# A selective scan in longer chains: units of 16 channels by 8 states over 1024 tokens, two halves in a row, with the B and C rows loaded once and ten product tiles

## The chip, the cores and the metric

The kernel runs on one core of one Trainium2 chip. The metric is the device time of one execution in microseconds (us); lower is better. The engines are named as in the profile: PE (TensorE, the matmuls), PEld (its weight loads), DVE (VectorE), ACT (ScalarE), POOL (GpSimd) and SP (SyncE, which here only issues DMAs).

## The reference

Four images of 64x64 tokens with 128 channels pass through four layers. The layer that matters here is the first, a selective scan: the tokens of an image are read in four orders (k = 0 to 3: by rows, by columns, and both backwards), and for each order, each of 256 channels and each of 16 states a recurrence runs over all 4096 tokens.

```python
xs    = stack([x0, x1, x0[..., ::-1], x1[..., ::-1]])      # 4 orders, 256 channels, 4096 tokens
delta = softplus(dts + dt_b)                               # one number per order, channel, token
A     = -exp(A_log)                                        # per order, channel, state
def step(h, t):
    x_t, d_t, B_t, C_t = t
    h = exp(d_t[..., None] * A) * h + (d_t * x_t)[..., None] * B_t[:, :, None, :]
    return h, einsum('bkdn,bkn->bkd', h, C_t)              # sum over 16 states
_, ys = scan(step, h0, (xs, delta, Bs, Cs))
ys    = ys + Ds * xs                                       # then the four orders are added up
```

After it come a layer norm, a gate and a projection, an MLP, and three more layers (attention, convolutions, neighbourhood attention with an MLP). They are called "the rest" below, and they are not changed.

## The kernel before

**Work of the scan.** `scan_inputs` makes `delta`, `du` = delta * x and the B and C rows of an image and stores them to DRAM, one block for each order and each of 8 chunks of 512 tokens. `selective_scan` then goes through an image: four orders, 8 chunks, two halves `hf` of the channels, four groups `j` of 4 states, and two units `pp`: 512 units in an image, 2048 in all. A unit holds 32 channels by 4 states on the 128 partitions, and two channel groups `g` side by side, each over 512 tokens. Its steps are:

- L468: SP loads `dt` and `du` (512 KB each, a row of a channel broadcast to its 4 states; four buffers each; one pair of tiles serves four units). L478: SP loads `b_rows` and `c_rows` (256 KB each, broadcast to 32 channels; four buffers each) for each `hf` and `j`.
- L485: POOL multiplies `dB = du * B`, 128x1024, into one of four buffers.
- L491: ACT takes the exponential, 128x512, into a PSUM tile `dA`, one for each `g`; there are three such tiles.
- L493: DVE runs the recurrence, `tensor_tensor_scan`, 128x512, for each `g`. It begins from zero in the first chunk of an order and from a column of the tile `state` in the others. The two scans of a unit have nothing to do with each other.
- The product with C. In 9 of 16 units (11 of 16 in the first image) the scan is written back into `dA` and DVE multiplies it into a product tile `hc` (L498), once for each `g`. In the others (`on_pool`, chosen by the tuple `ON_POOL`) the scan is written into `hc` and POOL multiplies in place, 128x1024 (L506), two units later in the program (`BEHIND`). There are six `hc` tiles.
- The last column of the scan is copied to `state` by ACT for the next chunk: twice in a unit of the first kind (L500), once in the second (L502), and not at all in the last chunk of an order.
- L539: PE sums the states with the matrix `pick`: four matmuls for each pair of units into a PSUM tile `py`. Only this frees an `hc` tile. After four pairs ACT copies `py` to `y_sum` (L549, L556) and issues its store (L552, L558).

**Order of the work.** Each engine works through its own list of instructions in order. The lists are made when the kernel is built, by a scheduler that plays the program through and takes, for each engine, what would be ready, by priority. The scan of image 0 runs beside `scan_inputs` of the later images, the scan of image n beside the rest of image n-1, and the rest of the last image runs alone at the end. The rest uses PE and ACT most, DVE a little, POOL hardly at all.

The lines that set the buffers of the scan:

```python
dB = pool.tile([128, 2, LC], F32, name="dB", bufs=4)
nc.gpsimd.tensor_mul(dB, dus[pp], mid(bt, 2))
hc = pool.tile([128, 2, LC], F32, name="hc", bufs=6)
dA = psum.tile([128, LC], F32, name="dA", bufs=3)
```

Of the kernel before, what the change touches and what calls it, by code (L numbers as in the profile page):

```python
# [45 lines left out]
NPR, NJS = 4, NS // 4  # L46
# [10 lines left out]
SCAN_FIRST = 10_000_000  # L57

# [63 lines left out]
def make_consts(ctx, tc):  # L122
# [9 lines left out]
    K.mhalf = pool.tile([128, 128], F32, name="mhalf")  # L132
    nc.gpsimd.memset(K.mhalf, -0.5)
# [143 lines left out]
def scan_inputs(tc, K, A, D, img):  # L277
# [5 lines left out]
    with ExitStack() as ctx:  # L283
# [12 lines left out]
        def steps(o, c):  # L296
# [26 lines left out]
            for b in range(2):  # L323
                k, first = o + 2 * b, 64 * b + 1 + R
                nc.scalar.dma_start(D.bc[img][k][c].rearrange("n w t -> w n t"), xdbl[first : first + 2 * NS, :])
                nc.scalar.dma_start(D.delta[img][k][c], deltas[b])
                du = pool.tile([128, ND, LC], F32, name="du")
                nc.gpsimd.tensor_mul(  # L328
                    du.rearrange("p d (a b) -> p d a b", b=H),
                    deltas[b].rearrange("p d (a b) -> p d a b", b=H), tk,  # L330
                )
                nc.sync.dma_start(D.du[img][k][c], du)
# [77 lines left out]
def make_scan(ctx, tc, K, A):  # L410
# [7 lines left out]
    S.A = load("A_log", [128, KD, NJS, NPR, 2])  # L418
    nc.scalar.activation(S.A, S.A, AF.Exp)
    nc.vector.tensor_scalar_mul(S.A, S.A, -1.0)  # L420
    ds4 = load("Ds", [128, ND, KD])
    total = big.tile([128, ND], F32, name="Dsum")
    nc.vector.tensor_reduce(total, ds4, AX.X, ALU.add)
    S.skip = big.tile([128, ND, 128], F32, name="skip_diag")
    for d in range(ND):
        nc.scalar.activation(S.skip[:, d, :], K.ident, AF.Copy, scale=total[:, d : d + 1])

    S.pick = big.tile([128, 32], F32, name="pick")
    nc.gpsimd.memset(S.pick, 1.0)
    for base, sign in ((0, 1), (3, -1)):  # L430
        nc.gpsimd.affine_select(
            S.pick, S.pick, [[-4 * sign, 32]], ALU.is_ge, 0.0, base=base, channel_multiplier=sign
        )
    S.unit = 0
    return S


def selective_scan(tc, K, S, D, img):

# [9 lines left out]
    for k in ORDER:  # L455
        back = k >= 2
        order = slice(None, None, -1) if back else slice(None)
        last = 0 if back else LC - 1
        state = pool.tile([128, NJS, NPR, 2], F32, name="state")
        for i in range(NCH):  # L460
            c = NCH - 1 - i if back else i
            for hf in range(2):
                dts, dus = [], []
                for pp in range(2):
                    rows = span(2 * hf + pp, 32)
                    for name, src, out in (("dt", D.delta, dts), ("du", D.du, dus)):
                        t = pool.tile([128, 2, LC], F32, name=name, bufs=4)
                        nc.sync.dma_start(  # L468
                            t.rearrange("p g t -> p (g t)"),
                            src[img][k][c][rows].rearrange("d g t -> d (g t)").unsqueeze(1).to_broadcast([32, 4, 2 * LC]),  # L470
                        )
                        out.append(t)
                py = []
                for j in range(NJS):

                    bt, ct = (pool.tile([128, LC], F32, name=name, bufs=4) for name in ("b_rows", "c_rows"))
                    for w, t in enumerate((bt, ct)):
                        nc.sync.dma_start(  # L478
                            t, D.bc[img][k][c][4 * j : 4 * j + 4, w, :].unsqueeze(0).to_broadcast([32, 4, LC])
                        )  # L480
                    hcs, made = [], []
                    for pp in range(2):
                        pr = 2 * hf + pp
                        dB = pool.tile([128, 2, LC], F32, name="dB", bufs=4)
                        nc.gpsimd.tensor_mul(dB, dus[pp], mid(bt, 2))  # L485
                        on_pool = S.unit % 16 in ON_POOL[img > 0]
                        S.unit += 1
                        hc = pool.tile([128, 2, LC], F32, name="hc", bufs=6)
                        for g in range(2):
                            dA = psum.tile([128, LC], F32, name="dA", bufs=3)  # L490
                            nc.scalar.activation(dA, dts[pp][:, g, :], AF.Exp, scale=S.A[:, k, j, pr, g : g + 1])  # L491
                            hg = hc[:, g, :] if on_pool else dA
                            nc.vector.tensor_tensor_scan(  # L493
                                hg[:, order], dA[:, order], dB[:, g, order],
                                0.0 if i == 0 else state[:, j, pr, g : g + 1], ALU.mult, ALU.add,
                            )
                            if not on_pool:
                                mm = nc.vector.tensor_mul(hc[:, g, :], dA, ct)  # L498
                                if i < NCH - 1:
                                    nc.scalar.copy(state[:, j, pr, g : g + 1], dA[:, last : last + 1])  # L500
                        if on_pool and i < NCH - 1:
                            nc.scalar.copy(state[:, j, pr, :], hc[:, :, last])  # L502
                        if on_pool:

                            def product(hc=hc, ct=ct, made=made):
                                made.append(nc.gpsimd.tensor_mul(hc, hc, mid(ct, 2)))  # L506

                            waiting.append((S.unit + BEHIND, product))
                        else:
                            made.append(mm)  # L510
                        hcs.append(hc)
                        settle(S.unit)

                    def total(k=k, c=c, hf=hf, j=j, hcs=hcs, made=made, py=py):
                        if j == 0:
                            py.append(psum.tile([128, LC], F32, name="py"))
                            before = pool.tile([128, LC], F32, name="y_before", bufs=3)
                            if k == 0:
                                for pp in range(2):
                                    nc.sync.dma_start(  # L520
                                        before[span(pp, 64), :],
                                        D.xc[img][c][span(2 * hf + pp, 32)].rearrange("d g t -> g d t"),
                                    )
                                nc.tensor.matmul(py[0], S.skip[:, hf, :], before, start=True, stop=False)
                            elif k >= 2:
                                nc.sync.dma_start(before, D.y_first[img][k % 2][c][:, hf, :])
                                nc.tensor.matmul(py[0], K.ident, before, start=True, stop=False)
                            if k == 2:
                                cols = pool.tile([128, NCH, RC, RC], F32, name="y_before", bufs=3)
                                nc.sync.dma_start(  # L530
                                    cols.rearrange("p c a b -> p c (a b)"),
                                    D.y_cols[img][:, :, c, hf].rearrange("c p x -> p c x"),
                                )
                                nc.tensor.matmul(
                                    py[0].rearrange("p (a c b) -> p a c b", a=RC, b=RC), K.ident,
                                    cols.rearrange("p c a b -> p a c b"), start=False, stop=False,
                                )
                        for q in range(4):
                            mm = nc.tensor.matmul(  # L539
                                py[0][32 * q : 32 * q + 32, :], S.pick, hcs[q // 2][:, q % 2, :],  # L540
                                start=(k == 1 and j == 0), stop=(j == NJS - 1),
                            )
                            if q == 0:
                                for m in made:
                                    after(tc, mm, m)
                        if j == NJS - 1:
                            y = pool.tile([128, LC], F32, name="y_sum")
                            if k == 3:
                                nc.scalar.copy(  # L549
# [5 lines left out]
                            else:  # L555
                                nc.scalar.copy(y, py[0])  # L556
                                to = D.y[img][c] if k == 2 else D.y_first[img][k % 2][c]
                                nc.scalar.dma_start(to[:, hf, :], y)  # L558

                    waiting.append((max([S.unit] + [w[0] for w in waiting]), total))  # L560
                    settle(S.unit)
    settle(S.unit + BEHIND)


# [299 lines left out]
def make_layer2(tc, K, A, D, pool):  # L864

    nc = tc.nc

    def fold(out, raw, rows, width):  # L870

# [885 lines left out]
```

## Time and profile before

| what | value |
|---|---|
| device time, median of 3 runs (lowest to highest) | 8911.95 us (8906.75 to 8919.55) |
| span of the profiled execution | 8926.7 us, 14.7 us above that median |
| busy: PE, DVE, ACT, POOL | 7138.8, 7119.8, 5642.5, 7048.6 us |
| first scan of image 0, 1, 2, 3 begins at | 125, 2202, 4080, 5942 us |
| last scan ends, rest of the last image alone | 7795 us, then to 8927 us |
| scans on DVE (L493) | 4096 |
| products on DVE (L498), on POOL (L506) | 2432, 832 |
| ACT copies of states (L500, L502) | 2128 of 158 ns, 728 of 190 ns |

A row of the table of groups reads: line, engine, operation, tiles written and read, shape, count, then the busy time with the mean of one instruction, then the idle time of the engine just before them with what ended most of it. A row of the table of stretches gives the stretch, its length, and the busy time of each engine in it. In the timeline "x2" joins two instructions that follow each other.

### The profile page before, as it was taken

To read this page: it belongs to the slowest core of one execution; us is meant where nothing else is said; L and a number is where in the kernel's file an instruction comes from. 1 tells how busy PE (TensorE), PEld (TensorE's weight loads), DVE (VectorE), ACT (ScalarE), POOL (GpSimd) and SP (SyncE) were. 2 spreads that over 40 slices of the span, in tenths; PEclk is the share of its full clock that TensorE was granted. 3 is DMA by queue.
4 is the path that set the end of the run, shared out by engine and by line. 5 is a ranking of instruction groups with operands and counts; after the bars stand their busy time and mean duration, and the time that the engine had idled before them with its cause. 6 is when DMAs were issued, how large, how long until landed. Compare 5 with 4: busy or idle time off the path is not lost. (4 is left out here: it accounts for less than half of the span.)

```text
span 8926.7 us, 101201 instructions
## 1 busy us (share of the span) xinstructions
PE 7138.8 (80%) x30116; PEld 2711.7 (30%) x30116; DVE 7119.8 (80%) x8483; ACT 5642.5 (63%) x11581; POOL 7048.6 (79%) x3064
## 2 busy tenths in 40 slices
PE   6835868687788997887788988777888888888987
PEld 2211213132332232333322232333322333343333
DVE  3888878888899989998899989988999889813433
ACT  5646767676576666667766666657766666654355
POOL 5988898989899989998899979987899889900000
PEclk8756868697799998888899998888899988999989
DMA  5777676777554546566444555565544555520020
GB/s 174 249 236 239 227 252 239 266 240 266 188 168 165 170 150 222 188 205 201 164 165 164 179 180 195 191 208 171 166 167 169 169 198 194 173 69 4 7 79 29
DMA packets 864124, 1581.89 MB, mean 177 GB/s; under 512 B 219702, under 2 KB 344781, under 8 KB 859214
## 3 DMA queue, kind: packets, MB, share of 16 engines
q1 hardware_dynamic: 733261, 1399.17, 47.0%
q10 hardware_dynamic: 130304, 176.19, 5.5%
q8 instruction: 240, 3.93, 0.2%
q14 instruction: 319, 2.61, 0.1%
HBM read 1280.47 MB, written 283.59 MB: 175 GB/s over the span
## 5 line engine op out<-in xcount | busy, mean ns | idle before, releaser
L485 POOL TENSOR_TENSOR dB<-du,b_rows 128x1024 f32<-128x1024 f32 x2048 | 4801.3, 2368 | 622.9 <-DVE hc L493 184.8
L491 ACT ACTIVATE dA<-dt,w_A_log 128x512 f32<-128x512 f32 x4096 | 2784.7, 690 | 636.5 <-DVE hc L493 353.1
L493 DVE TENSOR_TENSOR_SCAN dA<-dA,state,dB 128x512 f32<-128x512 f32 x2128 | 2634.8, 1272 | 231.0 <-ACT dA L491 136.3
L493 DVE TENSOR_TENSOR_SCAN hc<-dA,state,dB 128x512 f32<-128x512 f32 x1456 | 1802.5, 1268 | 263.6 <-PE py L539 117.2
L506 POOL TENSOR_TENSOR hc<-hc,c_rows 128x1024 f32<-128x1024 f32 x832 | 1969.3, 2367 | 52.7 <-issue 23.9
L498 DVE TENSOR_TENSOR hc<-dA,c_rows 128x512 f32<-128x512 f32 x2432 | 1567.9, 676 | 115.0 <-PE py L539 97.5
L539 PE MATMUL py<-hc,pick 128*32 128x512 f32 x8192 | 1244.7, 686 | 367.3 <-POOL hc L506 270.7
L500 ACT COPY state<-dA 128x1 f32<-128x1 f32 x2128 | 327.5, 158 | 1220.4 <-DVE hc L498 1211.8
L829 PE MATMUL pa<-e,l_v 128*128 128x512 f32 x2048 | 1062.0, 650 | 16.8 <-ACT e L785 16.2
L781 PE MATMUL pair<-l_g,l_f 32*128 32x512 f32 x2048 | 530.5, 667 | 198.3 <-ACT e L785 146.9
L785 ACT ACTIVATE e<-pair 128x1024 f32<-128x1024 f32 (+1 forms) x448 | 508.4, 1135 | 225.7 <-PE pair L781 220.3
L829 PEld LDWEIGHTS pa<-e,l_v 128*128 128x128 f32 x2048 | 374.2, 199 | 668.5 <-issue 621.1
L539 PEld LDWEIGHTS py<-hc,pick 128*32 128x32 f32 x8192 | 209.5, 116 | 1114.7 <-issue 476.7
L247 PE MATMUL ps<-band,w_conv_diag 128*128 128x504 f32 (+3 forms) x1152 | 503.5, 596 | 6.7 <-ACT delta L397 6.5
L1287 PE MATMUL pair<-table,ident 128*128 128x512 f32 x768 | 414.3, 665 | 111.4 <-ACT e L1297 79.1
L493 DVE TENSOR_TENSOR_SCAN dA<-dA,dB 128x512 f32<-128x512 f32 x304 | 356.2, 1213 | 76.2 <-POOL dB L485 57.4
L328 POOL TENSOR_TENSOR du<-delta,xc 128x1024 f32<-128x1024 f32 x128 | 335.4, 2630 | 52.0 <-ACT delta L397 45.3
L1297 ACT ACTIVATE e<-pair 128x1024 f32<-128x1024 f32 (+1 forms) x224 | 254.3, 1135 | 155.6 <-PE pair L1291 155.6
L201 PE MATMUL ps<-ident,ln_xn 128*128 128x128 f32 x512 | 134.2, 360 | 263.9 <-ACT ln_xn L198 214.3
L219 PE MATMUL ps<-xnT,w_fc_w 128*128 128x512 f32 x512 | 266.6, 656 | 62.9 <-ACT xnT L202 22.7
L233 PE MATMUL ps<-mlp_h,w_fc_w 128*128 128x512 f32 x512 | 275.8, 683 | 42.6 <-ACT mlp_h L226 42.6
L247 PEld LDWEIGHTS ps<-band,w_conv_diag 128*128 128x128 f32 x1152 | 221.6, 194 | 288.7 <-issue 260.4
(274 smaller groups left out, 8400.0 us busy)
## 6 DMA issues: line engine op xcount, KB each, us to landing
b_rows<-bc_dram SPq DMA_DIRECT2D x1024, 256.0 KB
c_rows<-bc_dram SPq DMA_DIRECT2D x1024, 256.0 KB
dt<-delta_dram SPq DMA_DIRECT2D x512, 512.0 KB
du<-du_dram SPq DMA_DIRECT2D x512, 512.0 KB
delta_dram<-delta ACTq DMA_DIRECT2D x128, 512.0 KB
du_dram<-du SPq DMA_DIRECT2D x128, 512.0 KB
table<-biasT_dram SPq DMA_DIRECT2D x72, 512.0 KB
y_first_dram<-y_sum ACTq DMA_DIRECT2D x128, 256.0 KB
```

What stands on the lines that cost most here:

```text
L247: mm = nc.tensor.matmul(out[:, r0 - row0 : r1 - row0, c0:c1], lhsT((dy + 1) * 3 + dx + 1), src[:, r0 + dy : r1 + dy, c0 + dx : c1 + dx], s ...
L328: nc.gpsimd.tensor_mul(du.rearrange("p d (a b) -> p d a b", b=H), deltas[b].rearrange("p d (a b) -> p d a b", b=H), tk,)
L485: nc.gpsimd.tensor_mul(dB, dus[pp], mid(bt, 2))
L491: nc.scalar.activation(dA, dts[pp][:, g, :], AF.Exp, scale=S.A[:, k, j, pr, g : g + 1])
L493: nc.vector.tensor_tensor_scan(hg[:, order], dA[:, order], dB[:, g, order], 0.0 if i == 0 else state[:, j, pr, g : g + 1], ALU.mult, ALU.add,)
L498: mm = nc.vector.tensor_mul(hc[:, g, :], dA, ct)
L506: made.append(nc.gpsimd.tensor_mul(hc, hc, mid(ct, 2)))
L539: mm = nc.tensor.matmul(py[0][32 * q : 32 * q + 32, :], S.pick, hcs[q // 2][:, q % 2, :], start=(k == 1 and j == 0), stop=(j == NJS - 1),)
L781: nc.tensor.matmul(ps[:, u, :], f[quad, t // 4, span(t % 4, 128)], g[quad, c, :], start=True, stop=True)
L785: made = nc.scalar.activation(e, ps, AF.Exp)
L829: nc.tensor.matmul(pa, v[:, 8 * q + t, :], es[q], start=(t == 0 and q == 0), stop=(t == 7 and q == 3),)
L1287: nc.tensor.matmul(ps[:, u, :], K.ident, t[:, u, :], start=True, stop=False)
```

## The change

The unit keeps its size, 128x1024, but takes another cut: 16 channels by 8 states on the partitions and 1024 tokens of one channel group in a row. The two scans of a unit are now two halves of one chain: the second begins from the last column of the first, read where the first scan wrote it (`dA` or `hc`), and one ACT copy to `state` stands at the end of a unit, in three of four chunks (there are now four chunks of 1024 tokens in an order). `dt` and `du` tiles are 1 MB, two buffers each, and serve four units as before. `b_rows` and `c_rows` are 512 KB, loaded once in a chunk for each half of the states, with as many buffers as are in use at one time (two). `ON_POOL` is read with the unit's number counted from one instead of zero. From the second image on, after its first 40 units, four more product tiles come from a pool of their own (`widen`). The matrix `pick` has two variants, `y` tiles hold one group of channels over 1024 tokens, and their blocks in DRAM follow; the stores of `y` of orders 3 and 2 and the loads of `y_cols` go in two DMAs of 64 partitions instead of one of 128. The constant `mhalf` moves into the function that uses it.

```diff
-NPR, NJS = 4, NS // 4
+NPR, NSUB, NSH = 4, 2, 2
+LONG = 2 * LC
+NLG = NT // LONG
+HC, MORE, DB = 6, 4, 4
...
+class Products:
+    def widen(self, pool):
+        self.wider, self.more, self.turn = pool, True, -40
+    def tile(self):
+        self.turn += 1
+        if self.more and self.turn > 0 and self.turn % (HC + MORE) < MORE:
+            return self.wider.tile([128, LONG], F32, name="hc", bufs=MORE)
+        return self.pool.tile([128, LONG], F32, name="hc", bufs=HC)
...
-                        t = pool.tile([128, 2, LC], F32, name=name, bufs=4)
+                            t = pool.tile([128, 2, LONG], F32, name=name)
...
-                    bt, ct = (pool.tile([128, LC], F32, name=name, bufs=4) for name in ("b_rows", "c_rows"))
+                            if pr == 0 and a == 0:
+                                rows[h] = [pool.tile([128, LONG], F32, name=m, bufs=2) for m in ("b_rows", "c_rows")]
...
+    def run(x):
+        S.unit += 1
+        on_pool = S.unit % 16 in ON_POOL[img > 0]
+        x.dB = pool.tile([128, LONG], F32, name="dB", bufs=DB)
+        nc.gpsimd.tensor_mul(x.dB, x.du, x.b)
+        x.hc = S.products.tile()
...
+        start = 0.0 if x.first else x.state
+        for part in range(2):
+            at = span(1 - part if x.back else part)
+            dA = psum.tile([128, LC], F32, name="dA", bufs=3)
+            nc.scalar.activation(dA, x.dt[:, at], AF.Exp, scale=x.scale)
+            h = x.hc[:, at] if on_pool else dA
+            nc.vector.tensor_tensor_scan(
+                h[:, order], dA[:, order], x.dB[:, at][:, order], start, ALU.mult, ALU.add
+            )
+            if not on_pool:
+                x.made.append(nc.vector.tensor_mul(x.hc[:, at], dA, x.c[:, at]))
+            start = h[:, last : last + 1]
+        if not x.final:
+            nc.scalar.copy(x.state, start)
...
-        for name, shape in (("delta", [128, ND, LC]), ("du", [128, ND, LC]), ("bc", [NS, 2, LC])):
+        for name, shape in (("delta", [128, ND, 2, LC]), ("du", [128, ND, 2, LC]), ("bc", [NS, 2, 2, LC])):
...
+                    S.products.widen(scan_ctx.enter_context(tc.tile_pool(name="ss_more", bufs=1)))
```

## The prediction

> **What bounds the kernel now.** I read the table of stretches first, cut where the first scan of each image and of each order begins, because the busy shares of the whole span mix the scan with the 1122 us in which the rest runs alone. Three of the twelve stretches of images 1 to 3:
>
> ```profile
> core 0: us, PE busy (x) PEld busy (x) DVE busy (x) ACT busy (x) POOL busy (x), PEclk, DMA share, GB/s
> 4080.00:4577.00 497.00, 399.44 (x1618) 171.55 (x1610) 435.60 (x553) 362.14 (x780) 426.25 (x184) 0.87 0.51 169
> 4577.00:5010.00 433.00, 387.56 (x1559) 114.17 (x1560) 403.14 (x430) 285.71 (x544) 428.19 (x186) 0.93 0.48 166
> 5010.00:5491.00 481.00, 418.97 (x1750) 151.44 (x1752) 428.97 (x500) 310.93 (x634) 425.02 (x184) 0.90 0.57 188
> ```
>
> In the second POOL works 428 of 433 us: POOL sets its length. In the others POOL has the same work but idles 56 to 71 us; DVE idles 52 to 61 us. So two engines are nearly full. Summed over images 1 to 3 (5603 us), DVE idles 577 and POOL 470 us. In image 0 (2077 us) POOL is busy 1866 and DVE 1718.
>
> The groups say what fills them:
>
> ```profile
> L485 POOL TENSOR_TENSOR dB<-du,b_rows 128x1024 f32<-128x1024 f32 x2048 | 4801.3, 2368 | 622.9 <-DVE hc L493 184.8
> L493 DVE TENSOR_TENSOR_SCAN dA<-dA,state,dB 128x512 f32<-128x512 f32 x2128 | 2634.8, 1272 | 231.0 <-ACT dA L491 136.3
> L493 DVE TENSOR_TENSOR_SCAN hc<-dA,state,dB 128x512 f32<-128x512 f32 x1456 | 1802.5, 1268 | 263.6 <-PE py L539 117.2
> L500 ACT COPY state<-dA 128x1 f32<-128x1 f32 x2128 | 327.5, 158 | 1220.4 <-DVE hc L498 1211.8
> ```
>
> POOL waits mostly for DVE (a `dB` tile comes free when its scan is done), so DVE is the later of the two outside the POOL-bound stretches. The waits of images 1 to 3 (2202 to 7805 us) show what holds DVE:
>
> ```profile
> DVE hc L493 <- PE py L539: 96.5, 59, 5.7
> DVE hc L493 <- ACT dA L491: 81.8, 58, 4.5
> DVE ps L943 <- ACT ps L939: 80.3, 20, 5.4
> DVE dA L493 <- ACT dA L491: 77.8, 65, 5.1
> DVE hc L498 <- PE py L539: 37.0, 30, 3.6
> DVE dA L493 <- POOL dB L485: 32.1, 24, 3.9
> ```
>
> 134 us are waits for a product tile, 160 for an exponential, 80 are the rest's own. Only 44 (32 and 12) are for POOL.
>
> **The part that I hold decisive: neighbours on DVE.** The timeline shows how closely DVE instructions follow each other:
>
> ```profile
> 3203.16 1.28 DVE L493 TENSOR_TENSOR_SCAN dA<-dA,state,dB 128x512 f32<-128x512 f32 x1
> 3204.53 0.69 DVE L498 TENSOR_TENSOR hc<-dA,c_rows 128x512 f32<-128x512 f32 x1
> 3205.14 1.28 DVE L493 TENSOR_TENSOR_SCAN dA<-dA,state,dB 128x512 f32<-128x512 f32 x1
> 3206.46 0.69 DVE L498 TENSOR_TENSOR hc<-dA,c_rows 128x512 f32<-128x512 f32 x1
> 3207.06 2.45 DVE L493 TENSOR_TENSOR_SCAN hc<-dA,state,dB 128x512 f32<-128x512 f32 x2
> 3209.43 2.44 DVE L493 TENSOR_TENSOR_SCAN dA<-dA,state,dB 128x512 f32<-128x512 f32 x2
> ```
>
> A product that reads the scan just in front of it starts 1.37 and 1.32 us after that scan started. Two independent scans start 1.19 us apart (2.37 for two): the second begins before the first has ended. Over the whole trace the medians are 1.325 us (251 dependent pairs) and 1.175 us (1116 scans followed by a product of another tile), so a dependent neighbour costs 0.15 us. The list before mostly has scan, scan, product, product, so few neighbours depend on each other. In the list of the changed kernel, as built, a scan is followed at once by its own product 1734 times instead of 251, and in units for POOL by the second half of its own chain 529 times instead of 0, because the second half needs the first. The second kind is not in the trace; the nearest row gives 1.325 against 1.19 us, 0.135 us, with 0 and 0.3 as ends. Images 1 to 3: (1289 - 120) x 0.15 + 441 x 0.135 = 175 + 60 = +235 us of DVE time. Image 0: (445 - 131) x 0.15 + 88 x 0.135 = +59 us.
>
> How much lies on the path: in the four stretches that POOL sets (2710, 4577, 6460, 7377), DVE idles about 30 us of 430 and 103 of the 235 us fall there; I take half as covered, -51. The cover is POOL's own 2.33 us per instruction; where a DVE stall opens it is gone, and all 103 count. In image 0 POOL is busier than DVE, and I count half, +30.
>
> A rule speaks against this term. The Trainium skill, "VectorE: DVE Perf Modes", section "The DRAIN you can't avoid", says that the next operation waits for the pipe to empty anyway and that a semaphore between chained operations costs nothing extra. By it the 235 and 59 us would be 0 and the sum 8837 us. The rows above disagree by 0.15 us in each pair, and I take the rows.
>
> **Product tiles.** Ten instead of six, after image 1's first 40 units: of the 134 us for tiles between 0 and all can go. Products and scans that carry a wait on PE fall from 1852 to 1435 in the lists, a fifth; I take half of the time, -67. Image 0 keeps six and its 83 us.
>
> **State copies.** ACT loses 2128 + 728 copies (466 us) and gains 1536 at 158 ns (243 us): -223 us. It gains 64 store issues of 0.52 and 64 of 0.33 us, +54. ACT is 73% busy in these images and idled 1371 us in front of the copies, so only what comes late to DVE counts: 160 us for exponentials and 22 for states in images 1 to 3. The three `dA` tiles do not become more, and a first half's tile is now held until its second half is scanned, so I take a quarter of the 160 and half of the 22, -51 (ends: 0, -182). Image 0: -15 of its 108. In the second half 1216 scans read their start from PSUM, which no row shows; a start from `state` against none costs 60 ns (1272, 1213), so +-60 ns, +-73 us; I take 0, as it is a pointer read in both.
>
> **Loads.** `dt` and `du` double to 1024 MB together (a row goes to 8 partitions instead of 4), B and C fall from 512 to 128 MB. By the trace's packet medians (2 KB 84, 4 KB 159, 8 KB 309 ns) over 16 engines the loads take 326 + 2531 = 2857 us instead of 1376 + 1303 = 2679, two points of a share of 0.53 (0.71 in image 0): hidden. But rows have no spare buffer. At each chunk the first new C tile waits for the last product of the old one, and behind it on SP's queue stand `dt` and `du`. Landing took 4.4 us in the median for 256 KB and 5.0 for 512 KB; DVE has about two units, 6 to 7 us, before it needs the tile. POOL needs the second B tile after two `dB`, 4.7 us. So 0 to 5 us at each of 48 chunks, 0 to 240; I take 1, near the lower end, as most is covered: +48, and +10 for the 16 of image 0.
>
> **Nothing.** Scans, products, exponentials, POOL multiplications and matmuls stay as many and as large. Two more 393 ns copies, two 213 ns selects and the moved constant lie before the first scan at 125 us; stores of `delta` and `du` in 2 KB packets add 18 us of DMA time over 2077. If the DMAs were full these would be bare. The rest after 7805 us stays.
>
> **Sum.** Images 1 to 3: 235 - 51 - 67 - 51 + 48 = +114. Image 0: 30 - 15 + 10 = +25. Together +139 us on the span of 8926.7, and on the median of 8911.95, which is 14.7 lower: 9051 us.
>
> **The rivals.**
> - *Faster: the stalls shrink by more than DVE gains.* If all waits for tiles, exponentials, states and POOL go (134 + 160 + 22 + 44 = 360) against +235, images 1 to 3 fall by 125: 8787 us. It decides from 235 us of stalls saved, 41% of DVE's 577 idle. For it: ten tiles, 223 us less on ACT. Against: 80 us are the rest's, and `dA` stays at three. Chance 0.32, 8700 to 8890.
> - *Much slower: the rows arrive late.* A full landing of 5 us at all 64 chunks costs 320 instead of 58: 9313 us. Against: the cover above. Chance 0.12, 9200 to 9450.
> - *No difference:* within 0.2% (18 us, about what a measurement of this kernel can tell from no change). The terms cancel, 8912 us. Chance 0.06.
> - *Forecast:* 8935 to 9200, chance 0.50.
>
> **The numbers.** Slower 0.50 + 0.12 = 0.62, same 0.06, faster 0.32. The range goes from 8820 to 9290: it leaves out about a tenth at either side. The forecast's own range is 8935 to 9200.
>
> **What would show it.** Right: DVE's product after its scan starts 1.33 us behind it in most pairs, second halves for POOL units likewise; DVE's waits on PE's `py` below 70 us in images 1 to 3; POOL waits more for DVE; the stretches that POOL set get longer than 433 us. Wrong: second halves start 1.19 us after the first; the images get shorter than 1862 us although DVE's neighbours cost 0.15 us each; or DVE and POOL wait for `c_rows` and `b_rows` for hundreds of microseconds.

## The result: slower by 8.6%, and the profile after

| kernel | device time, median (lowest to highest) | ratio to before, 95% interval |
|---|---|---|
| before | 8915.75 us (8906.75 to 8920.03) | 1 |
| changed | 9689.83 us (9676.61 to 9698.3) | 1.0862, 1.085 to 1.0875 |

The direction of the forecast was right and the size was wrong: +774 us instead of +139, outside the range of 8820 to 9290 us. The profiled execution has a span of 9693.4 us. Cut at the first scan of each image, the time went here (times from the trace, in us, counted, like the first scans in the table before the prediction, from a point 11 us before the first instruction):

| | first scan at | image 0 | images 1 to 3 | last scan at | from there to the end |
|---|---|---|---|---|---|
| before | 125 | 2077 | 5603 | 7804 | 1134 |
| changed | 178 | 2211 | 6164 | 8553 | 1151 |
| difference | +53 | +134 | +561 | +749 | +17 |

The views count from the first instruction itself. So every stretch here and in the prediction begins and ends some 11 us after the scan that it is named for, and the rest of the last image ran alone for 1133 us of the span before, not 1122. The differences are not touched by this.

The table of stretches for the same orders of image 2 as were shown of before. Columns: the stretch, its length, the busy time of each engine, the granted clock of PE, the DMA share and GB/s.

```profile
core 0: us, PE busy (x) PEld busy (x) DVE busy (x) ACT busy (x) POOL busy (x), PEclk, DMA share, GB/s
4457.00:4986.00 529.00, 413.39 (x1627) 178.21 (x1626) 436.68 (x557) 355.74 (x694) 426.08 (x184) 0.85 0.75 175
4986.00:5466.00 480.00, 391.75 (x1540) 116.67 (x1544) 422.54 (x434) 277.55 (x465) 429.58 (x186) 0.88 0.71 168
5466.00:5998.00 532.00, 429.07 (x1726) 152.06 (x1718) 437.94 (x489) 297.23 (x537) 424.93 (x183) 0.87 0.78 183
```

POOL has its 425 to 430 us of work as before, but the stretch that it filled (433 us) now takes 480. DVE works 423 of them. Neither engine is full any more. The DMA share rose from about 0.5 to 0.75, and the GB/s did not rise with it.

The waits of DVE and then of POOL in images 1 to 3 (2389 to 8553 us; columns: total, times, longest):

```profile
DVE hc L585 <- DMA c_rows<-bc_dram: 450.2, 52, 26.5
DVE hc L581 <- ACT dA L579: 90.9, 57, 8.3
DVE dA L581 <- POOL dB L571: 70.3, 28, 14.4
DVE dA L581 <- ACT dA L579: 44.3, 34, 5.6
```

```profile
POOL dB L571 <- DVE dA L581: 228.8, 77, 18.5
POOL dB L571 <- DMA du<-du_dram: 214.2, 77, 12.5
POOL dB L571 <- DMA b_rows<-bc_dram: 207.7, 47, 19.1
```

Both engines now wait for DMAs. DVE waits for C rows for 450 us in 52 waits, 8.7 us each, about once in each of the 48 chunks. POOL waits 422 us for `du` and B rows. Before, POOL waited 2.9 us for `du` and 2.4 us for B rows in these images. The waits for a product tile are gone from the top of DVE's list, as forecast.

The groups on the changed lines (columns as before: busy time, mean ns, idle time ahead with what ended most of it):

```profile
L571 POOL TENSOR_TENSOR dB<-du,b_rows 128x1024 f32<-128x1024 f32 x2048 | 4793.5, 2358 | 1228.3 <-DVE dA L581 319.7 <-DMA du<-du_dram 272.6 <-DMA b_rows<-bc_dram 239.0
L579 ACT ACTIVATE dA<-dt,w_A_log 128x512 f32<-128x512 f32 x4096 | 2798.3, 690 | 2423.7 <-DVE dA L581 1885.1 <-DVE hc L581 372.0 <-DMA dt<-delta_dram 44.0
L585 DVE TENSOR_TENSOR hc<-dA,c_rows 128x512 f32<-128x512 f32 x2432 | 1662.3, 687 | 713.5 <-DMA c_rows<-bc_dram 520.6 <-PE py L518 85.0 <-DVE dA L581 2.3
L581 DVE TENSOR_TENSOR_SCAN hc<-dA,hc,dB 128x512 f32<-128x512 f32 x832 | 1064.9, 1280 | 140.2 <-ACT dA L579 88.7 <-DVE hc L581 1.4
```

No instruction got slower by more than a few per cent (POOL 2368 to 2358 ns, the scan 1268 to 1280, the product 676 to 687). What changed is the idle time ahead of them. The timeline of DVE shows the neighbours that the prediction was about (columns: start, duration):

```profile
3209.08 1.29 DVE L581 TENSOR_TENSOR_SCAN dA<-dA,dB 128x512 f32<-128x512 f32 x1
3210.40 0.69 DVE L585 TENSOR_TENSOR hc<-dA,c_rows 128x512 f32<-128x512 f32 x1
3211.01 1.27 DVE L581 TENSOR_TENSOR_SCAN hc<-dA,state,dB 128x512 f32<-128x512 f32 x1
3212.39 1.28 DVE L581 TENSOR_TENSOR_SCAN hc<-dA,hc,dB 128x512 f32<-128x512 f32 x1
3213.59 1.27 DVE L581 TENSOR_TENSOR_SCAN dA<-dA,state,dB 128x512 f32<-128x512 f32 x1
```

A product starts 1.32 us after its own scan, a second half 1.38 us after its first half, and a scan of another chain 1.20 us after the scan in front of it. Over the whole trace the medians are 1.322 (1734 products), 1.379 (529 second halves) and 1.174 to 1.199 us for independent neighbours.

The last view is the page's table of DMA queues (columns: packets, MB, share of the span of 16 engines); q1 is the queue with the scan's loads, first before, then after:

```profile
q1 hardware_dynamic: 733261, 1399.17, 47.0%
```

```profile
q1 hardware_dynamic: 492621, 1533.28, 65.5%
```

Ten per cent more bytes in a third fewer packets took 18 points more of the DMA time. In the trace, the 8 KB packets of images 1 to 3 (`dt` and `du`) take 608 ns in the median. The 4 KB packets, now nearly all of B and C rows, take 261 ns; before, those were nearly all of `dt` and `du` and took 159. A load of `dt` lands 7.4 us after its issue instead of 4.7, `du` 10.9 instead of 6.0, B rows 9.5 instead of 4.1, C rows 13.3 instead of 4.4.

### The profile page after: what moved, and what is told of

Same layout as the page of the kernel before. It is cut to its first block, busy times and chain, and to the rows that moved or that the text cites. A ratio compares the mean times of both kernels' runs of the same rounds, so it can differ in the third digit from the quotient of the medians.

```text
span 9693.4 us, 96555 instructions
## 1 busy us (share of the span) xinstructions
PE 7334.1 (76%) x30116; PEld 2773.1 (29%) x30116; DVE 7319.6 (76%) x8483; ACT 5539.4 (57%) x10263; POOL 7055.0 (73%) x3066
## 3 DMA queue, kind: packets, MB, share of 16 engines
q1 hardware_dynamic: 492621, 1533.28, 65.5%
## 5 line engine op out<-in xcount | busy, mean ns | idle before, releaser
L571 POOL TENSOR_TENSOR dB<-du,b_rows 128x1024 f32<-128x1024 f32 x2048 | 4793.5, 2358 | 1228.3 <-DVE dA L581 319.7
L579 ACT ACTIVATE dA<-dt,w_A_log 128x512 f32<-128x512 f32 x4096 | 2798.3, 690 | 2423.7 <-DVE dA L581 1885.1
L585 DVE TENSOR_TENSOR hc<-dA,c_rows 128x512 f32<-128x512 f32 x2432 | 1662.3, 687 | 713.5 <-DMA c_rows<-bc_dram 520.6
L581 DVE TENSOR_TENSOR_SCAN dA<-dA,dB 128x512 f32<-128x512 f32 x1520 | 1931.8, 1272 | 112.3 <-ACT dA L579 70.2
L518 PE MATMUL py<-hc,pick 128*32 128x512 f32 x8192 | 1273.1, 697 | 444.4 <-POOL hc L592 250.8
L581 DVE TENSOR_TENSOR_SCAN dA<-dA,state,dB 128x512 f32<-128x512 f32 x912 | 1162.0, 1275 | 153.4 <-POOL dB L571 95.2
L581 DVE TENSOR_TENSOR_SCAN hc<-dA,hc,dB 128x512 f32<-128x512 f32 x832 | 1064.9, 1280 | 140.2 <-ACT dA L579 88.7
L868 PE MATMUL pa<-e,l_v 128*128 128x512 f32 x2048 | 1109.3, 675 | 52.6 <-ACT e L824 49.6
L581 DVE TENSOR_TENSOR_SCAN hc<-dA,state,dB 128x512 f32<-128x512 f32 x624 | 793.1, 1271 | 75.3 <-ACT dA L579 29.4
L820 PE MATMUL pair<-l_g,l_f 32*128 32x512 f32 x2048 | 555.1, 694 | 300.5 <-ACT e L824 213.7
L824 ACT ACTIVATE e<-pair 128x1024 f32<-128x1024 f32 (+1 forms) x448 | 507.9, 1134 | 269.3 <-PE pair L820 250.5
L820 PEld LDWEIGHTS pair<-l_g,l_f 32*128 32x128 f32 x2048 | 144.5, 195 | 660.4 <-ACT e L824 349.8
L189 DVE BATCH_NORM_STATS2 ln_stats<-x 128x6 f32<-128x128 f32 x512 | 110.7, 280 | 263.9 <-DMA x<-in_x 142.1
```

Of the source, the lines that this page charges most:

```text
L518: mm = nc.tensor.matmul(n.py[span(q, 32), :], S.pick[:, a, :], pair[g].hc[:, span(half)], start=(n.k == 1 and a == 0 and h == 0), stop=final,)
L571: nc.gpsimd.tensor_mul(x.dB, x.du, x.b)
L579: nc.scalar.activation(dA, x.dt[:, at], AF.Exp, scale=x.scale)
L581: nc.vector.tensor_tensor_scan(h[:, order], dA[:, order], x.dB[:, at][:, order], start, ALU.mult, ALU.add)
L585: x.made.append(nc.vector.tensor_mul(x.hc[:, at], dA, x.c[:, at]))
L820: nc.tensor.matmul(ps[:, u, :], f[quad, t // 4, span(t % 4, 128)], g[quad, c, :], start=True, stop=True)
```

## The experiments

The theory after the result: the DMAs are the cause, in two parts. The rows of `dt` and `du`, each sent to 8 partitions, come at half the rate that was assumed, and the B and C rows have no spare buffer, so that their late landing is bare. The rival is the prediction's own term: the dependent neighbours on DVE. Where a kernel sends `dt` and `du` rows in another pattern (`rows`, `span`), they are those of other channels than the computation needs; where the second half does not begin from the first, its chain is cut there. "Eight-fold" means that each row of `dt` and `du` goes to 8 partitions, "four-fold" to 4. "Over before" is the ratio less one, times 8920 us, about the time of the kernel before.

| run | edit | median us | ratio (95%) | over before |
|---|---|---|---|---|
| changed kernel | | 9689.83 | 1.0862 (1.0850 to 1.0875) | +769 |
| ten tiles alone | before | 8904.25 | 0.9969 (0.9956 to 0.9981) | -28 |
| eight-fold rows | before | 8985.59 | 1.0064 (1.0047 to 1.0081) | +57 |
| four-fold rows | changed | 9337.47 | 1.0450 (1.0433 to 1.0468) | +401 |
| spare rows, six tiles | changed | 9463.01 | 1.0596 (1.0574 to 1.0618) | +532 |
| six tiles | changed | 9778.93 | 1.0960 (1.0941 to 1.0978) | +856 |
| halves unchained | changed | 9656.62 | 1.0823 (1.0805 to 1.0841) | +734 |
| four-fold, spare rows, six tiles | changed | 9253.07 | 1.0362 (1.0344 to 1.0380) | +323 |
| the same, unchained | changed | 9151.93 | 1.0250 (1.0229 to 1.0271) | +223 |

**Ten tiles alone.** The kernel before with `Products` and `widen`, and the constant `mhalf` moved.

```diff
-                        hc = pool.tile([128, 2, LC], F32, name="hc", bufs=6)
+                        hc = S.products.tile()
```

> The kernel before with one part of the change alone: four more product tiles from the second image on. Theory (the loss comes from the loads and from dependent neighbours on VectorE, ten tiles help): DVE's 134 us of waits for product tiles in images 1 to 3 shrink to under 40, and the time falls by 30 to 80 us, to 8840 to 8890. Rival (tiles are off the path, POOL and ACT take over the wait): within 18 us of 8916.

Measured: 8904 us, 28 less than before by the ratio (17 to 39), between the theory and the rival. The tile waits went, as the theory has it, and DVE then waited for POOL instead, as the rival has it (columns as above; before these two lines were 32.1 and 12 us):

```profile
DVE dA L508 <- POOL dB L500: 88.4, 105, 2.8
DVE hc L508 <- POOL dB L500: 51.4, 70, 1.6
```

The scans ended 104 us earlier (7700 instead of 7804), but from there to the end it took 80 us longer. That second loss is followed up in the last experiments.

**Eight-fold rows in the kernel before.** The loads of `dt` and `du` take 16 rows, each sent to 8 partitions, instead of 32 rows to 4; bytes, packets and tiles stay.

```diff
-                    rows = span(2 * hf + pp, 32)
+                    rows = span(2 * (2 * hf + pp), 16)
-                            ....to_broadcast([32, 4, 2 * LC]),
+                            ....to_broadcast([16, 8, 2 * LC]),
```

> The kernel before, but each dt and du tile is read from 16 rows of 4 KB, each sent to 8 partitions, instead of 32 rows sent to 4 (other channels are read than the reference asks for). Theory A (the broadcast to 8 partitions makes the packets slow): 4 KB packets rise from 159 to about 250 to 300 ns, the DMA share of images 1 to 3 from 0.54 to above 0.7, and the time rises by 50 to 300 us. Theory B (the length of 8 KB or the layout in DRAM makes them slow): packets stay near 159 ns and the time stays within 30 us of 8916.

Measured: the 4 KB packets went from 159 to 261 ns and the share of q1 from 47.0% to 56.2%, at the same 1399 MB:

```profile
q1 hardware_dynamic: 733261, 1399.17, 56.2%
```

So it is the pattern, 16 rows to 8 partitions each instead of 32 rows to 4, that slows the packets, not the length of 8 KB and not the new layout. The number of rows and the number of copies changed together; which of the two matters is not shown. The total rose by 57 us only. In that kernel `b_rows` and `c_rows` have four buffers each, which would cover a late landing; that was not tested by itself.

**Four-fold rows in the changed kernel.**

```diff
-                                src[img][k][c][span(NSUB * pr + a, 16)]...to_broadcast([16, 8, 2 * LONG]),
+                                src[img][k][c][span(pr, 32)]...to_broadcast([32, 4, 2 * LONG]),
```

> The changed kernel, but each dt and du tile is read from 32 rows of 8 KB, each sent to 4 partitions, instead of 16 sent to 8 (other channels are read than the reference asks for). Theory A (broadcast to 8): 8 KB packets fall from about 600 to 310-350 ns, landing of the C rows from 12.6 to about 6 us, DVE's wait for them from 450 to under 150 us, the time from 9690 to 9200-9350. Theory B (8 KB packets or layout): the packets stay near 600 ns and the time near 9690.

Measured: 8 KB packets at 309 ns in the median, DMA share of images 1 to 3 0.56 instead of 0.77, and 368 us of the 769 gone. The bytes of q1 stay, and its share falls from 65.5% to

```profile
q1 hardware_dynamic: 492621, 1533.28, 48.6%
```

DVE's largest wait shrank but did not go away:

```profile
DVE hc L585 <- DMA c_rows<-bc_dram: 265.1, 43, 22.7
```

I had expected under 150. A C tile lands 9.1 us after its issue, against two units of cover, 6 to 7 us.

**Spare rows, and the tiles that pay for them.** There is no room for both four more product tiles and a second set of row tiles. So one kernel has six product tiles and, from image 1 on, takes the row tiles of every other chunk from the freed space; the other only drops the four product tiles.

```diff
+                                where = S.products.wider if S.products.more and i % 2 else pool
-                                rows[h] = [pool.tile(...
+                                rows[h] = [where.tile(...
```

> The changed kernel with six product tiles throughout, and the space of the other four used for a second set of B and C row tiles from the second image on, used by every other chunk. Theory (rows without a spare buffer cost the most): DVE's 450 us of waits for C rows and POOL's 208 us for B rows in images 1 to 3 fall below 100 together, and the time falls by 200 to 350 us to 9340-9490. Rival (the DMAs are so slow that another load, dt or du, comes last instead): the waits move to du and dt and the time stays above 9600.

```diff
-                    S.products.widen(scan_ctx.enter_context(tc.tile_pool(name="ss_more", bufs=1)))
```

> The changed kernel with six product tiles throughout. Theory (ten tiles remove waits for tiles, as they did in the kernel before, 28 us there): DVE's waits on PE's py in images 1 to 3 return to over 100 us, but waits for C rows are there anyway, so the time rises by 20 to 80 us to 9710-9770. Rival (the deeper product queue only holds C rows longer): the time falls or stays within 20 us of 9690.

Measured: without the four tiles the changed kernel loses 87 us more, a little over the expected 20 to 80, so in it they are worth about three times what they gave alone. Between the two kernels with six tiles, the spare rows bring 856 - 532 = 324 us. The waits for B and C rows in images 1 to 3 fall from 658 to 18 us; POOL still waits for `du`, which stays eight-fold:

```profile
POOL dB L570 <- DMA du<-du_dram: 299.1, 92, 20.9
```

**Halves unchained.** The second half begins from the same start as the first, so no scan on DVE reads the one in front of it.

```diff
-            start = h[:, last : last + 1]
+            ended = h[:, last : last + 1]
...
-            nc.scalar.copy(x.state, start)
+            nc.scalar.copy(x.state, ended)
```

> The changed kernel, but the second half of a unit begins from the state column like the first instead of from the first half's end (the chain over 1024 tokens is left out). The list then has 175 scans followed at once by a dependent instruction instead of 2263. Theory (each costs 0.14 us of DVE time, partly hidden where DVE waits for rows): the time falls by 100 to 250 us to 9440-9590, less than the 294 us of all pairs. Rival (DVE has idle time enough while the DMAs set the pace): the time stays above 9620.

Measured: dependent neighbours fell from 2263 to 175, and the total by 35 us. The scans did end 177 us earlier (8376 instead of 8553), but DVE's waits for `dB` grew to 240 us (86 in the changed kernel), it still waited 387 us for C rows, and from the last scan to the end it took 136 us longer:

```profile
DVE hc L585 <- DMA c_rows<-bc_dram: 386.7, 51, 16.0
DVE dA L581 <- POOL dB L571: 191.0, 104, 17.8
```

So the neighbours account for about 35 of the 769 us here, as the rival of this run said. The rest of their price lay under waits for DMAs, and some of it in the end that did not follow (below).

**Four-fold and spare rows together, then also unchained.**

```diff
-                                src[img][k][c][span(NSUB * pr + a, 16)]...to_broadcast([16, 8, 2 * LONG]),
+                                src[img][k][c][span(pr, 32)]...to_broadcast([32, 4, 2 * LONG]),
-                                rows[h] = [pool.tile(...
+                                rows[h] = [where.tile(...
```

> The changed kernel with dt and du read from 32 rows sent to 4 partitions each (other channels than the reference asks for) and with the spare set of row tiles in place of the four product tiles. Theory (the two effects add up where they are not the same wait): waits for C and B rows below 60 us together, the time 9120 to 9230, that is 100 to 220 below the four-fold run's 9337; what is left over 8933 is the dependent neighbours and image 0, which has no spare rows. Rival (spare rows bring nothing once the loads are quick): 9300 to 9360.

The second adds the edit of the unchained halves:

```diff
-            start = h[:, last : last + 1]
+            ended = h[:, last : last + 1]
...
-            nc.scalar.copy(x.state, start)
+            nc.scalar.copy(x.state, ended)
```

> As the run before in this list, with the chain left out too (the second half of a unit begins from the state column). Theory (eight-fold loads, rows without a spare and dependent neighbours are the three costs, and the fewer state copies help): 8880 to 8990, about the kernel before. Rival (a fourth cost is hidden, such as the later start of the first scan, 171 instead of 125 us, or du and dt with one tile of lead): above 9050.

Measured: 9253 and 9152 us, both above what was expected. With the DMA waits out of the way, cutting the chains shortens the scans of the four images from 7989 to 7751 us, by 238 us (the whole price of the neighbours, 235 + 59 us, was forecast for them), and the total by 100. So the neighbours are a second cost, which shows only when the rows are in time. The last kernel is still 223 us above the one before, and that is not resolved: the first scan is 44 us later, images 1 to 3 are 80 us longer (with six tiles DVE waits 164 us for product tiles), and the rest lags (below).

**What the end follows.** In three comparisons the scans ended 104 to 240 us earlier and the total followed by less than half. In the trace the rest of image 2 is the other candidate for the end: its last attention matmul (`po`) lies behind the last scan.

| kernel | last scan | last `po` of image 2 | end | end after the later of the two |
|---|---|---|---|---|
| before | 7804 | 7844 | 8938 | 1094 |
| changed | 8553 | 8607 | 9704 | 1097 |
| ten tiles alone | 7700 | 7812 | 8913 | 1101 |
| halves unchained | 8376 | 8558 | 9663 | 1105 |
| four-fold, spare rows | 8160 | 8172 | 9278 | 1106 |
| the same, unchained | 7920 | 8062 | 9162 | 1100 |

The end comes 1094 to 1106 us after the last `po` of image 2, whatever the scans do. Two variants of the kernel with ten tiles alone test this by moving products between POOL and DVE, in image 0 or in the later images.

```diff
-ON_POOL = ((1, 4, 7, 10, 13), (0, 2, 4, 6, 9, 11, 13))
+ON_POOL = ((1, 5, 9, 13), (0, 2, 4, 6, 9, 11, 13))
```

> The kernel before with the ten product tiles alone (8904 us), and in image 0 four products of 16 on POOL instead of five: 32 products of 2.4 us less on POOL (77 us of 1866 busy in 2077) and 64 of 0.68 us more on DVE (43 us on 1718). Theory: in image 0 POOL sets the pace, so image 0 gets 25 to 60 us shorter; the scans of the later images and the rest beside them both start earlier by that, so the total falls by as much: 8845 to 8880 us, tail after the last scan 1214 us as in the ten-tile kernel. Rival: image 0 is set by the scan inputs of the later images, or DVE becomes the later engine: image 0 stays within 15 us of 2080 and the total within 15 us of 8904.

```diff
-ON_POOL = ((1, 4, 7, 10, 13), (0, 2, 4, 6, 9, 11, 13))
+ON_POOL = ((1, 4, 7, 10, 13), (0, 3, 6, 8, 11, 14))
```

> The kernel before with the ten product tiles alone (8904 us), and in images 1 to 3 six products of 16 on POOL instead of seven: 96 products of 2.4 us less on POOL (232 us) and 192 of 0.68 us more on DVE (130 us). Theory: with ten tiles POOL is the later engine (DVE waits 140 us for dB there), but the attention of image 2 ends 118 us after the last scan already and sets the end as much as the scans do: the scans may end 0 to 60 us earlier, the tail after them gets longer by nearly as much, total 8885 to 8925 us. Rival 1, the scans alone set the end: the total follows the last scan one for one. Rival 2, DVE is the later engine: the scans end 40 to 130 us later, total 8925 to 9000 us.

Measured: fewer POOL products in image 0 gave 8858.61 us, ratio 0.9929 (0.9915 to 0.9942), the fastest kernel of this study, and fewer in images 1 to 3 gave 9023.55 us, ratio 1.0115 (1.0100 to 1.0131). Both totals lie in or near a bound that was written down, and both for another reason than was written. Image 0 did not get shorter but 71 us longer (2151; DVE's products wait 136 us for product tiles there instead of 60.5), and the last scan came 45 us later than with ten tiles alone. In the other run the scans ended 89 us earlier, not later, and the total was some 120 to 130 us longer (119 by the medians, 130 by the ratios). The stretches after the last scan, of ten tiles alone and of these two (image 0, later images), show why:

```profile
7700.00:8902.00 1202.00, 1025.28 (x4860) 476.92 (x4858) 358.75 (x567) 583.70 (x879) 0.00 (x0) 0.92 0.12 40
```

```profile
7745.00:8855.00 1110.00, 956.31 (x4443) 446.04 (x4440) 354.84 (x555) 562.07 (x846) 0.00 (x0) 0.92 0.12 38
```

```profile
7611.00:9012.00 1401.00, 1174.93 (x5788) 543.08 (x5788) 366.37 (x597) 634.73 (x958) 0.00 (x0) 0.92 0.11 35
```

PE has 1025, 956 and 1175 us of work left when the scans are done (965 before). The work of the rest that the scans' time no longer covers is done alone. The last `po` of image 2 is at 7770 in the first variant and at 7930 in the second, and the end comes 1097 and 1094 us later, as in the table. So the end follows the rest of image 2, and scans that finish earlier are worth nothing beyond that. What sets the pace of the rest beside the scans was not isolated.

**The pattern of the rows.** The last two runs ask why eight-fold rows are slow.

```diff
-                                ...rearrange("d g h t -> d (g h t)").unsqueeze(1).to_broadcast([16, 8, 2 * LONG]),
+                                ...rearrange("d g h t -> d (g h t)").unsqueeze(0).to_broadcast([8, 16, 2 * LONG]),
```

> The changed kernel with the same 16 rows of dt and du, each still sent to 8 partitions and in packets of 8 KB, but one row goes to every 16th partition instead of to 8 neighbours (so dt and du no longer match the channels of the other operands; only the time counts). Theory A, what slows the packets is that neighbouring partitions take the same row: 8 KB packets at 309 to 350 ns instead of 608, DMA share of images 1 to 3 near 0.55 instead of 0.77, total as with four-fold rows (9337 us), 9290 to 9390. Theory B, a row sent 8 times is slow however it is laid out: packets at 570 to 650 ns, share 0.75 or more, total 9650 to 9730.

The second has the B and C rows the other way round too (`unsqueeze(1)`, `[8, 16, LONG]`), with `pick` and `A_log` to match.

```diff
-                                        .unsqueeze(0).to_broadcast([16, 8, LONG]),
+                                        .unsqueeze(1).to_broadcast([8, 16, LONG]),
-    A["L0_conv_A_log"] = w.transpose(4, 6, 0, 2, 3, 5, 1)...
+    A["L0_conv_A_log"] = w.transpose(6, 4, 0, 2, 3, 5, 1)...
```

> The changed kernel with the whole unit laid out that way, states outside and channels inside on the partitions: dt and du rows go to every 16th partition, b_rows and c_rows rows to 16 neighbours each, and the matrix pick and the layout of A_log follow. Theory A: dt and du packets at 309 to 350 ns, the 4 KB packets of B and C slow instead (600 ns or more against 261), c_rows landing 10 to 25 us after its issue; total 9330 to 9550. Theory B: dt and du as in the changed kernel, total 9650 to 9850.

Measured: 12122 and 12107 us, ratios 1.3586 (1.3563 to 1.3609) and 1.3582 (1.3539 to 1.3625), far outside both theories. The 8 KB packets took 529 and 504 ns, between A and B. These runs do not decide the question, since they changed a second thing. In the changed kernel the landing of a `dt` load shows as sixteen events, 6.7 to 7.6 us after the issue. With the interleaved rows it shows as one event at 1.0 us and eight at 14 to 17 us. And the DMA share of images 1 to 3 stays at 0.57 although POOL waits for `du` more than for anything else (the line is of the whole run):

```profile
POOL dB L571 <- DMA du<-du_dram: 1437.5, 191, 49.0
```

So the loads queue while over 40% of the engines' time is free. The Trainium skill, "DMA: Bandwidth & Descriptors", section "Rules for kernel authors", says that an outermost dimension of fewer than 16 confines a DMA to at most that many engines. The eight events and the share of 0.57 agree with it; the trace does not name the engine of a packet. Why eight-fold rows are slow with all sixteen parts at work stays open.

## Why the prediction was wrong

- **Loads, the step that failed.** The sum took the 8 KB packet at 309 ns, from packets of another kind: 24 DMAs of the bias table, 12 stores in image 0 and 12 loads while the rest runs alone, none of them broadcast. So `dt` and `du` were to take 2531 us of DMA time and be "hidden". The 8 KB packets took 4707 us, at 608 ns in images 1 to 3, and in image 0 the DMA share went from 0.71 to 0.90 (that image got 134 us longer, +25 forecast). Shown by the runs with eight-fold rows in the kernel before and four-fold rows in the changed one, worth 368 us there.
- **Row reload, mis-sized and not independent of it.** It was put at about 1 us for each of 64 chunks, 58 us, with a top of 240 for 48. DVE waited 450 us for C rows and POOL 208 for B rows in images 1 to 3. The working had the mechanism (no spare tile, `dt` and `du` beside it on SP's queue) and judged it with landing times of the kernel before, 4.4 us for 256 KB and 5.0 for 512 KB (`dt`; `du` took 6.0), where 512 KB of C rows behind slower traffic took 13.3. Spare rows are worth 324 us. That DVE and POOL wait for `c_rows` and `b_rows` for hundreds of microseconds was the prediction's own last sign of being wrong.
- **Neighbours, right in size, wrong in place.** The distances from the start of a scan to the next start on DVE, summed where they are under 1.4 us (no wait between), rose by 238 us in images 1 to 3 (235 forecast) and by 77 in image 0 (59). But "the part that I hold decisive" had 184 + 30 us of it on the path, and only about 35 us of the total went away without it. So the forecast had the direction right mostly by luck: the term that gave it its sign is not the one that made most of the loss. What the Trainium skill says in "VectorE: DVE Perf Modes", section "The DRAIN you can't avoid", that a semaphore between chained operations costs nothing extra, is not borne out here: a neighbour that depends on the one in front cost 0.15 us in a pair of scan and product (1.322 against 1.174), 0.18 in a pair of scans (1.379 against 1.199), and cutting the chains saved 238 us of scan time once the rows were in time. The same section adds that an operation that is not "held" starts earlier, which the prediction left out; independent neighbours here do start before the one in front has ended (1.19 us apart at 1.27 us each).
- **Product tiles.** -67 was forecast. Alone they gave -28: the scans ended 104 us earlier, and then POOL and the rest of image 2 set the pace; in the changed kernel, where C rows come in bursts, losing them costs 87.
- **State copies.** DVE's waits for exponentials and states in images 1 to 3 went from 182 to 149 us, -33 against -51. ACT was busy for 65% of images 1 to 3 before (3668 of 5603 us); the prediction's 73% is the first stretch that it shows. The place of the time that ACT gained is plain in the group of L579: it waits 1885 us for DVE. No run tested this term alone.
- **Nothing, a term missed.** The first scan begins 53 us later. A chain of 1024 tokens needs two blocks of 512 from `scan_inputs`, so the first `dt` load is issued at 151.1 us instead of 104.6. That is 46 us read from the two traces; it was not tested by itself.
- **Rivals.** "Much slower: the rows arrive late" named the cause and priced it at 5 us a chunk; it was 8.7 us on DVE alone. "Faster" fell: the stalls for tiles and exponentials did shrink, and others of 870 us came on both engines.
- **The end.** The sum added every saving of the scans to the total. The table of last `po` matmuls shows that a saving there counts only as far as the rest of image 2 keeps up.

## What to carry to other kernels

Before a load is called hidden, take the packet time from a load with the same broadcast pattern, or bound it by twice the row that is at hand, and ask what the landing then does to the tile that has no spare buffer. A removed buffer and a slower load work together: each of the two, mended by itself, gave over 300 us here (368 and 324), and both 533 (856 - 323, with six tiles), less than the sum, because each covers part of the other. And before a saving on the busiest engine is counted, look for the second chain that ends just behind it; here it was 40 us away.

## What the runs showed of the hardware

- A DRAM row sent to 8 partitions in a DMA of 16 rows: 261 ns for 4 KB instead of 159, 608 ns for 8 KB instead of 309. Sent to 4 partitions, both ran at the faster figure. The B and C rows of the kernel before go to 32 partitions each, in another order, and ran at 84 ns for 2 KB, about half of 159 for half the bytes. So the number of copies alone does not decide. Nor is a packet's time its pattern's alone: the 4 KB packets of B and C rows in the changed kernel took 261 ns beside eight-fold loads and 204 beside four-fold ones.
- Turning the order of the broadcast from 16 x 8 to 8 x 16 made the whole program 25% slower for the same bytes (12122 against 9690 us), with the DMA share at 0.57.
- A scan that begins from a column in PSUM took 1288 ns in the mean (the 912 scans `dA<-dA,dB` behind the first chunks), against 1271 to 1280 from a column in SBUF and 1209 to 1213 from zero. The group's mean of 1272 mixes it with the 304 scans that begin from zero.
